# Two streams of a recurrent layer: the output product moved a step later, its result read out by ScalarE and added on GpSimd, the sums of x taken from accumulators

## Chip, cores and metric

The kernel runs on one core of one Trainium2 chip. The metric is the device time of one execution in microseconds. The work per core is divided over five engines with queues of their own, each served in order: TensorE (PE; its weight loads are PEld), VectorE (DVE), ScalarE (ACT), GpSimd (POOL) and SyncE (SP), which here issues the transfers.

## The reference

Sixteen images of 192 channels and 56 x 56 pixels (T = 3136 tokens) go through three recurrent layers and a graph convolution, each with a group norm in front and a residual sum behind. In float32, cut to what matters:

```python
# layers 0 to 2; gn is a group norm over 32 groups
xs = tokens(gn(x))                        # (B, T, C)
k, v, r = xs @ Wk.T, xs @ Wv.T, xs @ Wr.T
fwd = wkv_scan(-exp(w_decay), u, k, v)    # a ratio of two decaying sums along T
bwd = flip(wkv_scan(-exp(w_decay), u, flip(k), flip(v)))
h = sigmoid(r) * 0.5 * (fwd + bwd)
h = (h - mean(h)) * rsqrt(var(h) + eps) * ln_g + ln_b      # over the channels
x = x + image(h @ Wo.T)
# layer 3
xj = max(0, differences of gn(x) to the pixels two rows and two columns away)
x = x + gelu(batchnorm(concat(gn(x), xj) @ conv_w.T + conv_b))
```

The next layer's group norm needs the sums of x and of its squares, for each channel, over all tokens.

## The kernel before

**Tiles.** Images are taken in pairs: a tile of 128 partitions x 3 columns x 448 tokens holds a chunk of one pair (column 0 and 2: the first 128 channels of either image; column 1: the other 64 of both). T is seven chunks. Loops over the three columns go in the order 0, 2, 1.

**Two streams.** The eight pairs form two streams of four. While one stream goes backward through a layer (chunks 6 to 0), the other goes forward (chunks 0 to 6) through its own layer. `steps` is a list written out ahead: each step has at most one backward unit B and one forward unit A (or C, a chunk of the convolution). Chunk 6 of a backward pass stands alone (`backward_alone`), then five or six steps have both: `both_a_first` and five times `both_a` where the forward unit is one of a recurrent layer, `both_c` where it is one of the convolution. The seventh forward chunk follows in `forward_a` or `forward_c`. The plan holds 17 phases of one `both_a_first` and five `both_a` (85 in all), 42 `both_c`, 66 `forward_a`, 24 `backward_alone` and 14 `forward_c`.

**Order.** These functions write the order of instructions out by hand: every engine keeps the order in which they are issued there, and waits with semaphores for the data of others.

**A forward unit.** `a_keys` and `a_values` are products on TensorE, `a_exp` the exponential on ScalarE, `a_ekv` (L885) multiplies by it, `a_q` and `a_p` are scans on VectorE (L836) of the denominator and the numerator, `a_den` and `a_num` add the bonus term (L851, one instruction for columns 0 and 2 and one for column 1, both inputs in SBUF). Ln and Exp on ScalarE (L906, L909) invert the denominator, `a_y` (L913, GpSimd) multiplies. `save` copies a scan's last column for the next chunk (L847 on GpSimd, L845 on ScalarE).

**A backward unit.** `b_gate` and `b_exp` (L934) are the gate's product and exponential, `b_sigmoid` makes the gate of it. `b_q` and `b_p` are the scans the other way, `b_den` and `b_num` their bonus. After the inversion `b_mix` (L969 to L971, GpSimd, nine instructions, all with both inputs in SBUF) makes h. `b_squares` (L978, ScalarE) squares it into the slot of ek, `b_sums` (L985, L987, TensorE) sums h and its squares over channels, `b_rs1` to `b_rs3` make the inverse deviation, `b_spread` (L1009, TensorE) copies it to all partitions, `b_scale` (L1014, VectorE) multiplies h by it. Then the way out:

```python
    def b_x(run, c):
        wob, ps, xs = params[run.l][4], run.ps["o"], run.xb[c]
        for j in ORDER:
            xj = xs.t[:, j, :]
            V.scalar_tensor_tensor(xj, ps[j][:, 0:L], wob[:, column(j)], xj, ALU.add, ALU.add)
```

`b_out` (L591 to L600) is the output product, `b_x` (L1027) adds it and a bias to x and stores x to DRAM (`xd`), and `b_stats` (L722, L723) makes ScalarE pass over x twice, for its sums and those of its squares. `late` notes at which stage a backward chunk stands when its step has ended: 0 (mixed), 0.5 (summed), 1, 2. In `both_a` a chunk mixed in one step is scaled, projected and added in the next.

**Memory.** 33 slots in SBUF hold all tiles of chunk size; a freed slot goes to the end of a list, and the next tile takes the first of the list. A tile's first writer waits until the slot's last reader has ended. Seven PSUM banks are handed out the same way. `gap` and `begin_now` put the steps of the next layer's norm (`norm_sums`, L728, first) between.

Of the kernel before, what the change touches and what calls it, by code (L numbers as in the profile page):

```python
# [39 lines left out]
P = 128  # L40
# [433 lines left out]
def fast_path(ctx: ExitStack, tc: tile.TileContext, flag, x, wproj, wfold, wcfold, wconst, wgroup, sums, picks, vecs, out):  # L474
# [7 lines left out]
    keep = ctx.enter_context(tc.tile_pool(name="fkeep", bufs=1))  # L482
    row = ctx.enter_context(tc.tile_pool(name="frow", bufs=1))
    small = ctx.enter_context(tc.tile_pool(name="fsmall", bufs=4))
    dram = ctx.enter_context(tc.tile_pool(name="fdram", bufs=1, space=bass.MemoryType.DRAM))
    psum = ctx.enter_context(tc.tile_pool(name="fpsum", bufs=1, space=bass.MemoryType.PSUM))
    psconst = ctx.enter_context(tc.tile_pool(name="fpsconst", bufs=1, space=bass.MemoryType.PSUM))
# [6 lines left out]
    def name(s):  # L494
        ngen[0] += 1
        return f"{s}_{ngen[0]}"
# [34 lines left out]
    def column(j):  # L531
        return slice(j % 2, j % 2 + 1)
# [79 lines left out]
    def of(t):  # L612
        return lambda rows, j: t[rows, j, :]
# [100 lines left out]
            self.m, self.ml, self.q, self.p = {}, {}, {}, {}  # L714

    def new_stats():
        return small.tile([P, 2, 3, NL], F32, tag="stats", name=name("stats"))

    def chunk_stats(stats, xt, c):

        for j in ORDER:
            S.activation(junk, xt[:, j, :], AF.Identity, accum_out=stats[:, 0, j, c : c + 1])  # L722
            S.activation(junk, xt[:, j, :], AF.Square, accum_out=stats[:, 1, j, c : c + 1])  # L723


# [198 lines left out]
    def b_gate(run, c):  # L924
        product(run, "r", run.w[2], run.xb[c], c == NL - 1)
        if c == NL - 1:
            take_bias(run, "r", S, -1.0)

    def b_exp(run, c):
        ps, b = run.ps["r"], run.bias["r"]  # L930
        sg = run.sg[c] = Slot("sg")
        for j in ORDER:
            at = j * NL + c
            S.activation(  # L934
                sg.t[:, j, :], ps[j][:, 0:L], AF.Exp, bias=b[:, j, :], scale=-1.0, accum_out=run.chk[:, at : at + 1]
            )
            release(ps[j])
# [57 lines left out]
    def b_rs2(run, c):  # L995
        rs, st = run.rs[c], run.ps["st"]
        V.tensor_sub(rs[HI, :], st[HI, :L], rs[HI, :])  # L997
        release(st)

    def b_rs3(run, c):  # L1000
        rs = run.rs[c]
        S.activation(rs[HI, :], rs[HI, :], AF.Ln, bias=eps4[HI, :])
        S.activation(rs[HI, :], rs[HI, :], AF.Exp, scale=-0.5)  # L1003

    def b_spread(run, c):
        rs = run.rs.pop(c)
        ps = run.ps["rsb"] = banks("rsb")
        for j, rows in ((0, slice(64, 96)), (2, slice(96, P)), (1, HI)):
            PE.matmul(ps[j][:, :L], pick[rows, j, :], rs[rows, :], start=True, stop=True)  # L1009
# [5 lines left out]
            release(ps[j])  # L1015

    def b_out(run, c):
        h = run.h.pop(c)
        run.ps["o"] = banks("ops")
        project(run.ps["o"], params[run.l][5], of(h.t), L)  # L1020
        h.give()

    def b_x(run, c):
        wob, ps, xs = params[run.l][4], run.ps["o"], run.xb[c]
        for j in ORDER:
            xj = xs.t[:, j, :]
            V.scalar_tensor_tensor(xj, ps[j][:, 0:L], wob[:, column(j)], xj, ALU.add, ALU.add)  # L1027
            release(ps[j])
        nc.sync.dma_start(run.dst[c], xs.t)

    def b_stats(run, c):
        xs = run.xb.pop(c)
        chunk_stats(run.new, xs.t, c)
        if c == 0:
            require_all(run.chk, slice(0, NCHK))
            nxt = run.follow
            nxt.stats, nxt.src = run.new, run.dst
            nxt.xa[0] = xs
            begin_later(nxt)
        else:  # L1040
            xs.give()
# [163 lines left out]
    def add(u):  # L1205
        b_x(*u)
        unsummed.append(u)
        del late[u]

    def keys(f):  # L1210
        if f is not None:
            begin_now(f[1])
            if f[0] == "A":
                a_keys(*f[1:])
# [9 lines left out]
    def both_a(b, a, nback, nfront):  # L1224

        den = lambda: a[0].den[a[1]]
        l = of_stage(0.5)
        load_ahead(nback)
        load_ahead(nfront)
        store()  # L1230
        if nback is not None:
            b_gate(*nback[1:])
            b_exp(*nback[1:])
        b_q(*b)
        if l:
            b_rs2(*l)
            b_rs3(*l)
        b_sigmoid(*b)
        a_values(*a)
        if l:  # L1240
            b_spread(*l)
        b_p(*b)
        b_den(*b)
        invert(b[0].ek[b[1]])
        b_num(*b)
        b_mix(*b)
        if l:
            b_scale(*l)
            b_out(*l)
            late[l] = 2  # L1250
        a_ekv(*a)
        sum_up()
        keys(nfront)
        a_q(*a)
        if l:
            add(l)
        b_squares(*b, (0,))
        a_save(*a)
        exp_keys(nfront, (0, 2))
        b_squares(*b, (2,))  # L1260
        exp_keys(nfront, (1,))
        b_squares(*b, (1,))
        b_sums(*b)
        a_p(*a)
        gap()
        a_den(*a)
        b_rs1(*b)
        late[b] = 0.5
        invert(den())
        gap()  # L1270
        a_num(*a)
        a_y(*a)
        gap()

    def both_a_first(b, a, nback, nfront):

        den = lambda: a[0].den[a[1]]
        l = of_stage(0)
        load_ahead(nback)
        load_ahead(nfront)  # L1280
        store()
        a_values(*a)
        b_squares(*l, (0, 2))
        b_q(*b)
        b_sigmoid(*b)
        b_p(*b)
        b_den(*b)
        invert(b[0].ek[b[1]])
        b_num(*b)
        b_mix(*b)  # L1290
        a_ekv(*a)
        b_squares(*l, (1,))
        if nback is not None:
            b_gate(*nback[1:])
            b_exp(*nback[1:])
        b_sums(*l)
        deviation(l)
        a_q(*a)
        keys(nfront)
        spread_and_scale(l)  # L1300
        b_squares(*b, (0,))
        a_save(*a)
        exp_keys(nfront)
        b_squares(*b, (2, 1))
        b_sums(*b)
        a_p(*a, V)
        a_den(*a)
        b_rs1(*b)
        ln(den())
        add(l)  # L1310
        a_num(*a)
        late[b] = 0.5
        exp_minus(den())
        a_y(*a)

    def both_c(b, a, nback, nfront):

# [48 lines left out]
    def forward_a(a, nback, nfront):  # L1366
        l = next(iter(late), None)
        den = lambda: a[0].den[a[1]]
        a_values(*a)
        load_ahead(nback)  # L1370
        ahead = nfront is not None and nfront[1].begun
        if ahead:
            load_ahead(nfront)
        if l and late[l] == 2:
            add(l)
            l = None
        if l and late[l] == 0:
            squares_and_sums(l)
            b_rs1(*l)
            late[l] = 0.5  # L1380
        if l and late[l] == 0.5:
            b_rs2(*l)
            b_rs3(*l)
            late[l] = 1
        if l:
            b_spread(*l)
        elif ahead:
            keys(nfront)
        store()
        a_q(*a)  # L1390
        a_save(*a)
        if ahead and not l:
            exp_keys(nfront)
        a_den(*a)
        gap()
        invert(den())
        a_ekv(*a)
        gap()
        if l:
            b_scale(*l)  # L1400
            if ahead:
                keys(nfront)
                exp_keys(nfront)
            b_out(*l)
            late[l] = 2
        sum_up()
        if nback is not None:
            b_gate(*nback[1:])
        a_p(*a)
        gap()  # L1410
        if l:
            add(l)
            sum_up()
        a_num(*a)
        a_y(*a)
        if nback is not None:
            b_exp(*nback[1:])
        if not ahead:
            load_ahead(nfront)
            keys(nfront)  # L1420
            exp_keys(nfront)
# [231 lines left out]
```

## Time and profile before

| what | us |
|---|---|
| median of 3 runs (lowest, highest) | 5382.33 (5381.34, 5385.62) |
| the profiled execution | 5382.77 |
| its span, first to last instruction | 5381.0 |
| VectorE busy in it | 5014.9 (93%) |
| TensorE busy (ends are modelled) | 4629.7 (86%) |
| ScalarE busy | 3681.2 (68%) |
| GpSimd busy | 2770.3 (51%) |
| granted TensorE clock, mean | 0.916 |

A row of the groups says line, engine, operation, output and inputs, shapes and count, then the busy time, the mean ns of one, and the idle time ahead with what ended it. A row of the timeline says start and length in us, engine, line, operation and count; in brackets the idle time ahead and its releaser. A row of the windows gives, for a stretch, its length and each engine's busy time with its number of instructions, in the order PE, PEld, DVE, ACT, POOL, then the granted clock, DMA's share and GB/s.

### The profile page before, as it was taken

What the parts mean: (1) busy time and instruction counts of PE and PEld (TensorE: products, weight loads), DVE (VectorE), ACT (ScalarE), POOL (GpSimd) and SP (SyncE); (2) the same over time, 40 slices, a digit from 0 to 9 for tenths busy, and PEclk for the clock granted to TensorE, in tenths of its full rate; (3) what the DMA queues carried; (4) which work ended last, traced back from release to release, by engine and by line L of the source; (5) the groups of instructions that cost most, each with busy time, mean ns of one, the idle gap of its engine ahead of it and who ended that gap; (6) DMA issues with size and microseconds to landing.
All of it is one profiled execution on the core that took longest, in us unless ns stands there. A gap on an engine that the chain in (4) does not pass through costs nothing. (4 is left out here: it accounts for less than half of the span.)

```text
span 5381.0 us, 50984 instructions
## 1 busy us (share of the span) xinstructions
PE 4629.7 (86%) x15206; PEld 1498.6 (28%) x15206; DVE 5014.9 (93%) x6556; ACT 3681.2 (68%) x7035; POOL 2770.3 (51%) x2164
## 2 busy tenths in 40 slices
PE   6888988989798898888979888888888988898897
PEld 2222322223232222222323222222222222222222
DVE  6989999999999999999999999999999999999996
ACT  6777667767676676676667767667667566676673
POOL 1555555645454465555444455555535455555463
PEclk8989989989899898998989989999898998999898
DMA  5222212124243212213425121221343312222233
GB/s 149 78 80 72 85 66 88 63 90 140 87 131 89 82 63 73 74 67 105 144 87 150 56 74 67 85 74 62 111 139 94 111 56 74 70 77 80 77 102 115
DMA packets 314271, 482.42 MB, mean 90 GB/s; under 512 B 66432, under 2 KB 306688, under 8 KB 313984
## 3 DMA queue, kind: packets, MB, share of 16 engines
q1 hardware_dynamic: 312832, 477.59, 27.9%
q8 instruction: 123, 2.02, 0.2%
q10 hardware_dynamic: 1152, 1.48, 0.1%
q14 instruction: 164, 1.34, 0.1%
HBM read 324.83 MB, written 154.14 MB: 89 GB/s over the span
## 5 line engine op out<-in xcount | busy, mean ns | idle before, releaser
L913 POOL TENSOR_TENSOR p<-p,q 128x1344 f32<-128x1344 f32 x168 | 510.1, 3037 | 887.8 <-ACT q L909 472.1
L969 POOL TENSOR_TENSOR ekv<-ekv,ek 128x448 f32<-128x448 f32 x504 | 618.2, 1227 | 677.1 <-DVE p L1014 304.9
L836 DVE TENSOR_TENSOR_SCAN p<-fdecays,cp,ekv 128x448 f32<-128x448 f32 x864 | 928.5, 1130 | 7.2 <-POOL p L913 4.5
L836 DVE TENSOR_TENSOR_SCAN q<-fdecays,cq,ek 128x448 f32<-128x448 f32 x864 | 929.2, 1131 | 1.9 <-PE st L987 0.2
L971 POOL TENSOR_TENSOR p<-p,sg 128x448 f32<-128x448 f32 x504 | 599.4, 1189 | 54.5 <-ACT cq L845 10.7
L970 POOL TENSOR_TENSOR p<-p,ekv 128x448 f32<-128x448 f32 x504 | 600.6, 1192 | 39.5
L847 POOL COPY cp<-p 128x3 f32<-128x3 f32 x271 | 196.4, 725 | 686.9 <-DVE p L836 454.3
L978 ACT ACTIVATE ek<-p 128x448 f32<-128x448 f32 x504 | 283.6, 573 | 259.4 <-POOL p L971 257.5
L591 PE MATMUL ops<-p,fwo 128*128 128x448 f32 x336 | 223.5, 755 | 275.3 <-DVE p L1014 275.2
L866 ACT ACTIVATE ek<-k,k 128x448 f32<-128x448 f32 x504 | 292.1, 630 | 243.0 <-PE k L594 216.4
L723 ACT ACTIVATE fjunk<-x 128x448 f32<-128x448 f32 x672 | 387.6, 577 | 21.1
L722 ACT ACTIVATE fjunk<-x 128x448 f32<-128x448 f32 x672 | 384.6, 572 | 14.6
L851 DVE SCALAR_TENSOR_TENSOR q<-ek,fcc,q 128x896 f32<-128x896 f32 x336 | 337.1, 1043 | 51.1 <-ACT cq L845 51.1
L1009 PE MATMUL rsb<-rs,fpicks 32*128 32x448 f32 (+1 forms) x1008 | 335.8, 594 | 48.8 <-ACT rs L1003 46.7
L1027 DVE SCALAR_TENSOR_TENSOR x<-ops,fwob,x 128x448 f32<-128x448 f32 x504 | 315.9, 674 | 52.2 <-PE ops L594 27.1
L851 DVE SCALAR_TENSOR_TENSOR ek<-ek,fcc,q 128x896 f32<-128x896 f32 x336 | 361.6, 1117 | 2.8 <-POOL chk L919 2.8
L851 DVE SCALAR_TENSOR_TENSOR ekv<-ekv,fcc,p 128x896 f32<-128x896 f32 x336 | 330.4, 1024 | 1.2
L934 ACT ACTIVATE sg<-r,r 128x448 f32<-128x448 f32 x504 | 311.9, 624 | 15.8 <-PE r L594 10.4
L885 DVE SCALAR_TENSOR_TENSOR ekv<-v,v,ek 128x448 f32<-128x448 f32 x504 | 312.9, 677 | 0.0
L1014 DVE TENSOR_TENSOR p<-p,rsb 128x448 f32<-128x448 f32 x504 | 281.5, 614 | 31.1 <-PE rsb L1009 31.0
L851 DVE SCALAR_TENSOR_TENSOR p<-ekv,fcc,p 128x896 f32<-128x896 f32 x336 | 293.4, 913 | 10.0 <-POOL cp L847 9.7
L906 ACT ACTIVATE q<-q 128x1344 f32<-128x1344 f32 x168 | 222.4, 1324 | 90.4 <-DVE q L851 65.9
(232 smaller groups left out, 11795.3 us busy)
## 6 DMA issues: line engine op xcount, KB each, us to landing
x<-xd SPq DMA_DIRECT2D x240, 672.0 KB, 5.5
xd<-x SPq DMA_DIRECT2D x168, 672.0 KB, 4.0
x<-in_x_dram SPq DMA_DIRECT2D x320, 224.0 KB, 4.6
x<-in_x_dram SPq DMA_DIRECT2D x320, 112.0 KB, 4.6
out_dram<-ml SPq DMA_DIRECT2D x112, 224.0 KB, 2.3
ring<-xd SPq DMA_DIRECT2D x112, 168.0 KB, 5.3
wkv<-in_wfold_dram SPq DMA_DIRECT2D x24, 640.0 KB, 5.5
out_dram<-ml SPq DMA_DIRECT2D x112, 112.0 KB, 2.3
```

The source lines that it names most:

```text
L722: S.activation(junk, xt[:, j, :], AF.Identity, accum_out=stats[:, 0, j, c : c + 1])
L723: S.activation(junk, xt[:, j, :], AF.Square, accum_out=stats[:, 1, j, c : c + 1])
L836: V.tensor_tensor_scan(s.t[:, j, order], dec[:, column(j)].to_broadcast([P, L]), data.t[:, j, order], init, ALU.mult, ALU.add)
L851: by_channel(lambda js, i: V.scalar_tensor_tensor(dst.t[:, js, :], e.t[:, js, :], cc[:, i : i + 1], state.t[:, js, :], ALU.mult, ALU.add))
L885: V.scalar_tensor_tensor(e.t[:, j, :], ps[j][:, 0:L], b[:, j, :], run.ek[c].t[:, j, :], ALU.add, ALU.mult)
L913: G.tensor_mul(run.h[c].t, run.h[c].t, den.t)
L934: S.activation(sg.t[:, j, :], ps[j][:, 0:L], AF.Exp, bias=b[:, j, :], scale=-1.0, accum_out=run.chk[:, at : at + 1])
L969: G.tensor_mul(y.t[:, j, :], y.t[:, j, :], den.t[:, j, :])
L970: G.tensor_add(h.t[:, j, :], h.t[:, j, :], y.t[:, j, :])
L971: G.tensor_mul(h.t[:, j, :], h.t[:, j, :], sg.t[:, j, :])
L1009: PE.matmul(ps[j][:, :L], pick[rows, j, :], rs[rows, :], start=True, stop=True)
L1027: V.scalar_tensor_tensor(xj, ps[j][:, 0:L], wob[:, column(j)], xj, ALU.add, ALU.add)
```

## The change

In `both_a`, a chunk that was mixed in one step is scaled at the end of the next and projected a step later still (stage 1.5): `b_out` runs early in that step, `b_evict` has ScalarE read the product from PSUM into h, with the bias, and accumulate its sums; `b_add` has GpSimd add h to x, store x, and add the sums of the old x, which `run.stats` holds, to the new sums. The last `both_a` of a phase does this for two chunks. `both_a_first` scales its chunk at the end and leaves it at stage 1.5. In the other steps `b_x` stays on VectorE, with an accumulator output for the sums of x. `b_stats` makes squares only. `both_a`, `both_a_first` and `forward_a` are put in a new order. Statistics get a pool of seven buffers of their own (four before, shared).

```diff
+    def chunk_squares(stats, xt, c):
+        for j in ORDER:
             S.activation(junk, xt[:, j, :], AF.Square, accum_out=stats[:, 1, j, c : c + 1])
...
     def b_x(run, c):
+        run.h.pop(c).give()
...
-            V.scalar_tensor_tensor(xj, ps[j][:, 0:L], wob[:, column(j)], xj, ALU.add, ALU.add)
+            V.scalar_tensor_tensor(
+                xj, ps[j][:, 0:L], wob[:, column(j)], xj, ALU.add, ALU.add, accum_out=run.new[:, 0, j, c : c + 1]
+            )
...
+    def b_evict(run, c):
+        wob, ps, h = params[run.l][4], run.ps["o"], run.h[c].t
+        for j in ORDER:
+            S.activation(
+                h[:, j, :], ps[j][:, 0:L], AF.Identity, bias=wob[:, column(j)], accum_out=run.new[:, 0, j, c : c + 1]
+            )
+            release(ps[j])
+
+    def b_add(run, c):
+        h, xs = run.h.pop(c), run.xb[c]
+        G.tensor_add(xs.t, xs.t, h.t)
+        h.give()
+        nc.sync.dma_start(run.dst[c], xs.t)
+        new = run.new[:, 0, :, c : c + 1]
+        G.tensor_add(new, new, run.stats[:, 0, :, c : c + 1])
...
     def b_stats(run, c):
         xs = run.xb.pop(c)
-        chunk_stats(run.new, xs.t, c)
+        chunk_squares(run.new, xs.t, c)
...
+    def add_evicted(u):
+        b_add(*u)
+        unsummed.append(u)
+        del late[u]
```

`both_a` after the change, whole:

```python
        den = lambda: a[0].den[a[1]]
        l, o = of_stage(0.5), of_stage(1.5)
        last = nback is None
        load_ahead(nback)
        load_ahead(nfront)
        store()
        b_q(*b)
        b_sigmoid(*b)
        a_values(*a)
        b_p(*b)
        sum_up()
        b_rs2(*l)
        b_rs3(*l)
        a_ekv(*a)
        b_out(*o)
        b_den(*b)
        invert(b[0].ek[b[1]])
        b_num(*b)
        b_mix(*b)
        if last:
            b_spread(*l)
            b_scale(*l)
        else:
            b_gate(*nback[1:])
        b_evict(*o)
        if not last:
            b_exp(*nback[1:])
        b_squares(*b, (0,))
        a_q(*a)
        a_save(*a)
        keys(nfront)
        if last:
            b_out(*l)
        b_squares(*b, (2,))
        exp_keys(nfront)
        a_p(*a)
        gap()
        if not last:
            b_spread(*l)
        a_den(*a)
        gap()
        ln(den())
        a_num(*a)
        b_squares(*b, (1,))
        exp_minus(den())
        b_sums(*b)
        b_rs1(*b)
        add_evicted(o)
        if last:
            b_evict(*l)
            add_evicted(l)
        else:
            b_scale(*l)
            late[l] = 1.5
        a_y(*a)
        gap()
        late[b] = 0.5
```

The other two functions, where their order changes:

```diff
     def both_a_first(b, a, nback, nfront):
...
         deviation(l)
+        keys(nfront)
         a_q(*a)
-        keys(nfront)
-        spread_and_scale(l)
         b_squares(*b, (0,))
         a_save(*a)
         exp_keys(nfront)
-        b_squares(*b, (2, 1))
-        b_sums(*b)
+        b_spread(*l)
+        b_squares(*b, (2,))
         a_p(*a, V)
         a_den(*a)
+        ln(den())
+        a_num(*a)
+        b_squares(*b, (1,))
+        exp_minus(den())
+        b_sums(*b)
         b_rs1(*b)
-        ln(den())
-        add(l)
-        a_num(*a)
+        b_scale(*l)
+        late[l] = 1.5
+        a_y(*a)
         late[b] = 0.5
-        exp_minus(den())
-        a_y(*a)
...
     def forward_a(a, nback, nfront):
...
+        if l:
+            if late[l] == 0.5:
+                b_rs2(*l)
+                b_rs3(*l)
+            b_spread(*l)
+            a_den(*a)
+            invert(den())
+            sum_up()
+            a_ekv(*a)
+            b_scale(*l)
+            b_out(*l)
+            if nback is not None:
+                b_gate(*nback[1:])
+            if ahead:
+                keys(nfront)
+                exp_keys(nfront)
+            a_p(*a)
+            a_num(*a)
             add(l)
             sum_up()
```

More of the change, by code (lines that the diff above doesn't have):

```diff
@@ L484, in fast_path @@
     small = ctx.enter_context(tc.tile_pool(name="fsmall", bufs=4))
+    statistics = ctx.enter_context(tc.tile_pool(name="fstats", bufs=7))
     dram = ctx.enter_context(tc.tile_pool(name="fdram", bufs=1, space=bass.MemoryType.DRAM))
@@ L716, in new_stats @@
     def new_stats():
-        return small.tile([P, 2, 3, NL], F32, tag="stats", name=name("stats"))
+        return statistics.tile([P, 2, 3, NL], F32, tag="stats", name=name("stats"))
     def chunk_stats(stats, xt, c):
@@ L722, in chunk_stats @@
             S.activation(junk, xt[:, j, :], AF.Identity, accum_out=stats[:, 0, j, c : c + 1])
+        chunk_squares(stats, xt, c)
+    def chunk_squares(stats, xt, c):
+        for j in ORDER:
             S.activation(junk, xt[:, j, :], AF.Square, accum_out=stats[:, 1, j, c : c + 1])
@@ L1017, in b_out @@
     def b_out(run, c):
-        h = run.h.pop(c)
         run.ps["o"] = banks("ops")
-        project(run.ps["o"], params[run.l][5], of(h.t), L)
-        h.give()
+        project(run.ps["o"], params[run.l][5], of(run.h[c].t), L)
     def b_x(run, c):
+        run.h.pop(c).give()
         wob, ps, xs = params[run.l][4], run.ps["o"], run.xb[c]
@@ L1226, in both_a @@
         den = lambda: a[0].den[a[1]]
-        l = of_stage(0.5)
+        l, o = of_stage(0.5), of_stage(1.5)
+        last = nback is None
         load_ahead(nback)
@@ L1230, in both_a @@
         store()
-        if nback is not None:
-            b_gate(*nback[1:])
-            b_exp(*nback[1:])
         b_q(*b)
-        if l:
-            b_rs2(*l)
-            b_rs3(*l)
         b_sigmoid(*b)
         a_values(*a)
-        if l:
-            b_spread(*l)
         b_p(*b)
+        sum_up()
[3 more added lines that the diff above has]
+        b_out(*o)
         b_den(*b)
@@ L1246, in both_a @@
         b_mix(*b)
-        if l:
+        if last:
+            b_spread(*l)
             b_scale(*l)
-            b_out(*l)
-            late[l] = 2
-        a_ekv(*a)
-        sum_up()
-        keys(nfront)
-        a_q(*a)
-        if l:
-            add(l)
-        b_squares(*b, (0,))
-        a_save(*a)
-        exp_keys(nfront, (0, 2))
+        else:
+            b_gate(*nback[1:])
+        b_evict(*o)
+        if not last:
+            b_exp(*nback[1:])
+        b_squares(*b, (0,))
+        a_q(*a)
+        a_save(*a)
+        keys(nfront)
+        if last:
+            b_out(*l)
         b_squares(*b, (2,))
-        exp_keys(nfront, (1,))
-        b_squares(*b, (1,))
-        b_sums(*b)
+        exp_keys(nfront)
         a_p(*a)
         gap()
+        if not last:
+            b_spread(*l)
         a_den(*a)
-        b_rs1(*b)
-        late[b] = 0.5
-        invert(den())
-        gap()
-        a_num(*a)
+        gap()
+        ln(den())
[3 more added lines that the diff above has]
+        b_sums(*b)
+        b_rs1(*b)
+        add_evicted(o)
+        if last:
+            b_evict(*l)
+            add_evicted(l)
+        else:
+            b_scale(*l)
+            late[l] = 1.5
         a_y(*a)
         gap()
+        late[b] = 0.5
     def both_a_first(b, a, nback, nfront):
@@ L1297, in both_a_first @@
         deviation(l)
+        keys(nfront)
         a_q(*a)
-        keys(nfront)
-        spread_and_scale(l)
         b_squares(*b, (0,))
@@ L1303, in both_a_first @@
         exp_keys(nfront)
-        b_squares(*b, (2, 1))
-        b_sums(*b)
+        b_spread(*l)
+        b_squares(*b, (2,))
         a_p(*a, V)
         a_den(*a)
+        ln(den())
+        a_num(*a)
+        b_squares(*b, (1,))
+        exp_minus(den())
+        b_sums(*b)
         b_rs1(*b)
-        ln(den())
-        add(l)
-        a_num(*a)
+        b_scale(*l)
+        late[l] = 1.5
+        a_y(*a)
         late[b] = 0.5
-        exp_minus(den())
-        a_y(*a)
     def both_c(b, a, nback, nfront):
@@ L1380, in forward_a @@
             late[l] = 0.5
[L1381 to L1387, printed above, removed]
+        if not l and ahead:
             keys(nfront)
@@ L1391, in forward_a @@
         a_save(*a)
[L1392 to L1398, printed above, removed]
-        if l:
+        if l:
+            if late[l] == 0.5:
+                b_rs2(*l)
+                b_rs3(*l)
+            b_spread(*l)
+            a_den(*a)
+            invert(den())
+            sum_up()
+            a_ekv(*a)
             b_scale(*l)
+            b_out(*l)
+            if nback is not None:
+                b_gate(*nback[1:])
             if ahead:
@@ L1403, in forward_a @@
                 exp_keys(nfront)
[L1404 to L1411, printed above, removed]
+            a_p(*a)
+            a_num(*a)
             add(l)
             sum_up()
-        a_num(*a)
+        else:
+            if ahead:
+                exp_keys(nfront)
+            a_den(*a)
+            gap()
+            invert(den())
+            a_ekv(*a)
+            gap()
+            sum_up()
+            if nback is not None:
+                b_gate(*nback[1:])
+            a_p(*a)
+            gap()
+            a_num(*a)
         a_y(*a)
```

## The prediction

> **What bounds the kernel now.** I read the page's busy totals first, then a table of windows one step long, then the timeline of VectorE, GpSimd and ScalarE inside one step, and last the waits.
>
> ```profile
> PE 4629.7 (86%) x15206; PEld 1498.6 (28%) x15206; DVE 5014.9 (93%) x6556; ACT 3681.2 (68%) x7035; POOL 2770.3 (51%) x2164
> ```
> ```profile
> 453.60:478.90 25.30, 22.41 (x80) 6.94 (x78) 25.24 (x31) 19.16 (x36) 15.20 (x12) 1.00 0.17 56
> ```
>
> The second line is one steady step of `both_a`: 25.30 us, in which VectorE works 25.24 and TensorE 22.41. The plan holds 17 phases with one `both_a_first` and five `both_a` steps each, so 102 of the 168 backward chunks pass there; elsewhere (42 `both_c`, 17 forward steps after a phase, `backward_alone`) chunks keep the old way out. So in `both_a` a VectorE microsecond is a microsecond of the kernel. The next fence is one such step, VectorE with GpSimd between, in order of time:
>
> ```profile
> 408.35 1.72 DVE L851 SCALAR_TENSOR_TENSOR ek<-ek,fcc,q 128x896 f32<-128x896 f32 x2
> 409.99 1.74 DVE L851 SCALAR_TENSOR_TENSOR ekv<-ekv,fcc,p 128x896 f32<-128x896 f32 x2
> 412.86 1.14 POOL L969 TENSOR_TENSOR ekv<-ekv,ek 128x448 f32<-128x448 f32 x1 [3.34 <-DVE p L1014]
> ...
> 418.16 1.84 DVE L1027 SCALAR_TENSOR_TENSOR x<-ops,fwob,x 128x448 f32<-128x448 f32 x3
> 419.92 3.22 DVE L836 TENSOR_TENSOR_SCAN p<-fdecays,cp,ekv 128x448 f32<-128x448 f32 x3
> ...
> 422.32 1.14 POOL L971 TENSOR_TENSOR p<-p,sg 128x448 f32<-128x448 f32 x1
> 423.06 1.95 DVE L851 SCALAR_TENSOR_TENSOR q<-ek,fcc,q 128x896 f32<-128x896 f32 x2
> ```
>
> Read: `b_den`, `b_num`, then GpSimd's nine-instruction mix (412.86 to 423.46, 10.60 us), then the sum that is to leave VectorE, then `a_p` and `a_den`. `a_den` begins where the mix ends, and overlaps only its last 0.4 us. What an overlap costs is seen once per phase, where `both_a_first` meets the mix of the step ahead:
>
> ```profile
> 571.00 3.25 DVE L851 SCALAR_TENSOR_TENSOR ek<-ek,fcc,q 128x896 f32<-128x896 f32 x2
> 574.17 3.51 DVE L851 SCALAR_TENSOR_TENSOR ekv<-ekv,fcc,p 128x896 f32<-128x896 f32 x2
> ...
> 571.78 1.99 POOL L969 TENSOR_TENSOR ekv<-ekv,ek 128x448 f32<-128x448 f32 x1
> 573.85 1.40 POOL L970 TENSOR_TENSOR p<-p,ekv 128x448 f32<-128x448 f32 x1
> 575.33 1.87 POOL L971 TENSOR_TENSOR p<-p,sg 128x448 f32<-128x448 f32 x1
> ```
>
> The same four instructions that take 3.30 us free (408.35 to 411.65) take 6.61 (571.00 to 577.61): **3.3 us lost**, on both engines. Last, a wait for a slot, in the first phase:
>
> ```profile
> 252.83 3.23 DVE L836 TENSOR_TENSOR_SCAN p<-fdecays,cp,ekv 128x448 f32<-128x448 f32 x3 [2.00 <-POOL p L913]
> ```
>
> The scan takes its data from no GpSimd product `p`: it waits because its output slot was last read by the previous step's `a_y`. The steps of that phase take up to 29.6 us.
>
> **What the skill says.** The Trainium skill, "SBUF — State Buffer", Who interferes with whom: a VectorE instruction with two SBUF inputs contends with a GpSimd instruction that reads SBUF; one with a single SBUF input does not. The trace agrees: scans (decays lie in PSUM) and L1027 (PSUM plus `x`) keep their time under the mix, the four above double. "Perfetto Trace Analysis", Optimizing Scalar/DVE Operations, warns that moving work between GpSimd and VectorE might not help for that reason. The same page, Identifying Performance Opportunities, takes equal bubbles as a possible sign of too few buffers; the 2.00 us agree. "VectorE: DVE Perf Modes", Two Vector instructions with no wait between them: an accumulator output makes a second instruction; no run here shows its price.
>
> **The change, part by part.**
>
> *VectorE.* 102 x 3 instructions L1027 go. Start to start the three take 1.76 us (418.16 to 419.92), so a step falls from 25.32 (401.27 to 426.59) to 23.56 if nothing else happens.
>
> *ScalarE.* 306 evictions come; nearest row L934 (PSUM in, bias, accumulator): 624 ns plus a 196 ns readout, 0.62 from start to start. 504 identities of L722 go, 0.70 each with readout. In `both_a` that is level (19.2 us of ScalarE per step, cover over 4 us); elsewhere it saves 2.1 us per chunk on ScalarE.
>
> *GpSimd.* 102 additions of 128x1344, like L913 3.04 us, and 102 of 128x3 (L919: 0.20). Per step 15.2 + 3.2 = 18.4 us.
>
> *TensorE.* Same count. `b_out` uses a product scaled a step earlier; its wait on the scaling (2.92 us at 412.31) goes, and the four projections (4.5 us each), spread (2.0) and sums (2.15) make 22.2: it stays below VectorE.
>
> *SP.* The store of `xd` now waits for the addition, some 4 us into the next step, and that step's loads queue behind it. Landing takes about 5 us and TensorE wants the keys' input at about 14: hidden.
>
> *The order.* This decides. Between `b_num` and `a_den` VectorE had scale 1.59, ekv 1.78, `a_q` 3.14, sum 1.76 and `a_p` 3.14. Now scale is at the end, ekv ahead of `b_den`, the sum gone: 6.28 are left. From the start of `b_den`, the mix still begins at +4.51 (Ln and Exp, 408.35 to 412.86) and lasts to +15.11, but `a_den` comes at 1.64 + 1.66 + 6.28 = **+9.58, five mix instructions too early**. `a_den` and `a_num`, four instructions, meet it in full: +3.3, less the 0.21 that `a_den` already lost. Step: 23.56 - 0.21 + 3.3 = **26.65**, 1.33 over today.
>
> *Slots.* `h` lives a step longer, so of the 33 slots some two to six are free where three to nine were. Following the free list, first in first out, the first backward scan of the second and of the third `both_a` step of a phase gets the slot of `ek`, whose last reader is the previous step's sums on TensorE; all of VectorE's step is queued behind that scan. New step: q 3.27, p 3.16, rs 0.65, ekv 1.78, so `b_den` at 8.86, mix from 13.37; it loses some 2.2 to the four (three of its instructions took 5.42 instead of 3.5) and ends at 26.2. Square, sums and their end cost 1.73 more (423.46 to 425.19): the scan starts at **27.9**, past VectorE's 26.65. In the other steps the slot comes from the mix or earlier and is free in time. `b_p` waits for the addition (mix end + 4.2; wanted at + 5.0) and ekv for `a_y` (+ 7.5; wanted + 8.8): both just hidden. In the first phase two scans wait for `a_y` instead: 26.2 + 7.6 = 33.8 against 29.2 now.
>
> *Sum over `both_a`.* 16 phases x (2 x 2.6 + 2 x 1.33 + 1.2 for the last step, where scale sits between and four still meet the mix) = 145; first phase about 12. **+157.**
>
> *Around it.* `both_a_first`: sum out 1.76, `a_den` now meets the mix's last instruction (0.5): -1.3 x 17 = -22. Forward step and `backward_alone`: at 549.59 to 553.79 sums of `x` hold the next layer's norm up for 4.2 us; half of them go (-2.1), and `a_num` ahead of the last sum covers 0.9 of its two waits on TensorE (1.1 and 0.75); one contention of `a_den` there (2.56 us at 532.36) stays in another form: -3 x 17 = -51, bounds 0 and -85. 198 remaining L1027 get accumulators: below nothing has no reason; above, ScalarE's 0.19 each, 38; mostly hidden: +10. ScalarE's relief in `both_c`: 0 to -20, take -5.
>
> Total 157 - 22 - 51 + 10 - 5 = **+89** on the profiled execution's 5382.77 (span 5381.0; median of the runs 5382.33, the same within 0.5): **5472 us**.
>
> **The rivals.**
>
> *The port costs little (faster).* If `a_den` and `a_num` passed the mix free, a step would be 23.56, or 26.2 - 2.2 + 1.73 = 25.7 in the two that wait for sums, or 24.1 for the mix alone: 2 x 0.4 - 3 x 1.2 = -2.8 per phase, -48, with the surroundings' -68 about -115: **5268**. For it: only the two-input instructions are touched. Against: 571.00. The point from which it decides: at under some 1.4 us lost per step in place of 3.3 the whole is faster.
>
> *VectorE alone counts.* No contention, no slot wait: 102 x 1.76 + 68 = -248, **5135**. Against it: the 2.00 us slot wait.
>
> *Deeper starvation.* If a lower granted clock makes the sums later, or the additions push `a_y` into `b_den`, another 1.5 us in each of 85 steps: **5600**. For: by the layout TensorE idles some 4 us ahead of the sums' second half, and steps with a granted clock of 0.93 (428.3 to 453.6) hold 23.7 us of TensorE in place of 22.4. Against: v, wanted at 7.08, would come by about 5.
>
> *It doesn't do what it says:* excluded, 306 instructions leave VectorE.
>
> **How the numbers follow.** Main case 0.66, deeper starvation 0.10, port cheap 0.16, VectorE alone 0.03, ends cancelling 0.05. About 0.2% (11 us) can be told from no change. Slower 0.76, same 0.05, faster 0.19. Main alone: 5390 to 5550 (transitions' bounds, contention 2.4 to 3.5 us). The range leaves out most of the faster cases and the far end of starvation: 5340 to 5575.
>
> **What would show it.** VectorE steps near 26.7 and 27.9; `a_den` and `a_num` together near 6.6 us beside a mix of over 12; a wait of the first backward scan on TensorE's sums, about 1.3 us, in about 34 steps; less wait of the norm on ScalarE's sums. Steps below 25.3, or `a_den` pairs near 3.3, would make it wrong.

## The result: 5838.59 us, slower than forecast

The changed kernel takes **5838.59 us** (5837.69 to 5839.36, four runs) beside 5381.84 for the kernel before on the same chip: ratio 1.085, 95% interval 1.0831 to 1.0869. The forecast was 5472, with 5575 as its upper end: the sign was right, the size was not. Of a loss of 457 us, 89 were worked out.

The page's line of busy times, and the windows row of one steady step of `both_a` (columns as explained above):

```profile
PE 4870.6 (83%) x15206; PEld 1531.7 (26%) x15206; DVE 5208.3 (89%) x6448; ACT 3504.7 (60%) x6639; POOL 3116.8 (53%) x2368
```
```profile
468.50:499.74 31.24, 26.15 (x80) 7.60 (x78) 27.60 (x28) 18.55 (x35) 18.58 (x15) 0.95 0.22 67
```

VectorE has fewer instructions than before and is busy for 193 us more; in a step it works 27.60 us and stands still for 3.6. Before, a step was 25.30 with 25.24 busy. All 17 phases show it: no step of `both_a` is under 31.2. In the table a step is the time from the end of one `a_num` to the end of the next, in the profiled execution:

| us | before | after | difference, all |
|---|---|---|---|
| `both_a`, the first four of a phase (68) | 25.53 | 31.40 | +399 |
| `both_a`, the last (17) | 25.55 | 31.25 | +97 |
| forward step after a phase (17) | 18.76 | 17.15 | -27 |
| `backward_alone` with `both_a_first` (17) | 45.49 | 43.34 | -37 |
| other forward steps (42) | 12.90 | 13.67 | +32 |
| stretches with the convolution (6) | 201.96 | 200.75 | -7 |

The sum is +457. The timeline of VectorE at the end of a step, from `a_den` on, and of GpSimd beside it, first of before (the copy and `a_num`), then of after:

```profile
423.40 1.05 POOL L847 COPY cp<-p 128x3 f32<-128x3 f32 x1
424.93 1.73 DVE L851 SCALAR_TENSOR_TENSOR p<-ekv,fcc,p 128x896 f32<-128x896 f32 x2
```

```profile
467.92 3.21 DVE L856 SCALAR_TENSOR_TENSOR q<-ek,fcc,q 128x896 f32<-128x896 f32 x2
474.71 4.52 DVE L856 SCALAR_TENSOR_TENSOR p<-ekv,fcc,p 128x896 f32<-128x896 f32 x2 [3.58 <-POOL cp L852]
479.15 1.67 DVE L1019 TENSOR_TENSOR p<-p,rsb 128x448 f32<-128x448 f32 x3
```
```profile
468.79 1.86 POOL L976 TENSOR_TENSOR p<-p,sg 128x448 f32<-128x448 f32 x1
470.61 1.52 POOL L974 TENSOR_TENSOR ekv<-ekv,ek 128x448 f32<-128x448 f32 x1
...
473.42 1.13 POOL L976 TENSOR_TENSOR p<-p,sg 128x448 f32<-128x448 f32 x1
474.49 0.19 POOL L852 COPY cp<-p 128x3 f32<-128x3 f32 x1
474.64 3.05 POOL L1049 TENSOR_TENSOR x<-x,p 128x1344 f32<-128x1344 f32 x1
477.64 1.05 POOL L1053 TENSOR_TENSOR stats<-stats,stats 128x3 f32<-128x3 f32 x1
479.40 3.04 POOL L918 TENSOR_TENSOR p<-p,q 128x1344 f32<-128x1344 f32 x1 [0.71 <-DVE p L856]
```

Read: `a_den` runs beside the mix and ends at 471.13. `a_num` could follow, but it writes over the scan p, and the scan's last column must first be saved for the next chunk. GpSimd does that (L852, 0.19 us), in its order behind the mix, which ends at 474.55. So VectorE waits 3.58 us for a copy of three columns. Then the addition to x, next in GpSimd's queue, starts with `a_num` (474.64 and 474.71), and the two instructions of `a_num` take 4.52 us in place of 1.73. In the list of waits, first of before, then of after (total, times, longest):

```profile
DVE p L851 <- POOL cp L847: 9.7, 31, 1.2
```
```profile
DVE p L856 <- POOL cp L852: 283.5, 118, 3.6
```

The dependence was there before, too, and cost 9.7 us in all, 8.3 of them in the other forward steps. In `both_a`, `a_p` ended about when the mix did, so the copy came to a GpSimd that was just free and ran under `a_den` (423.40 to 424.45). After, 273 of the 283.5 us lie in the 85 steps of `both_a`. Over all chunks the page's groups of costly instructions show `a_num` at 1614 ns (913 before):

```profile
L856 DVE SCALAR_TENSOR_TENSOR p<-ekv,fcc,p 128x896 f32<-128x896 f32 x336 | 529.1, 1614 | 283.5 <-POOL cp L852 283.5
```

### The profile page after: what moved, and what is told of

It reads as the page before. It is cut to its first block, busy times and chain, and to the rows that moved or that the text cites. A ratio compares the mean times of both kernels' runs of the same rounds, so it can differ in the third digit from the quotient of the medians.

```text
span 5837.3 us, 51306 instructions
## 1 busy us (share of the span) xinstructions
PE 4870.6 (83%) x15206; PEld 1531.7 (26%) x15206; DVE 5208.3 (89%) x6448; ACT 3504.7 (60%) x6639; POOL 3116.8 (53%) x2368
## 5 line engine op out<-in xcount | busy, mean ns | idle before, releaser
L856 DVE SCALAR_TENSOR_TENSOR p<-ekv,fcc,p 128x896 f32<-128x896 f32 x336 | 529.1, 1614 | 283.5 <-POOL cp L852 283.5
L976 POOL TENSOR_TENSOR p<-p,sg 128x448 f32<-128x448 f32 x504 | 641.3, 1272 | 46.1 <-ACT sg L914 7.9
L852 POOL COPY cp<-p 128x3 f32<-128x3 f32 x271 | 70.8, 261 | 878.0 <-DVE p L841 606.5
L1014 PE MATMUL rsb<-rs,fpicks 32*128 32x448 f32 (+1 forms) x1008 | 387.7, 676 | 172.2 <-ACT rs L1008 112.6
L850 ACT ACTIVATE cq<-q 128x3 f32<-128x3 f32 x312 | 62.6, 201 | 691.3 <-DVE q L841 691.2
L856 DVE SCALAR_TENSOR_TENSOR q<-ek,fcc,q 128x896 f32<-128x896 f32 x336 | 416.6, 1279 | 51.5 <-ACT cq L850 50.9
L728 ACT ACTIVATE fjunk<-x 128x448 f32<-128x448 f32 x672 | 385.4, 573 | 19.1 <-issue 1.2
L992 PE MATMUL st<-p,fsums 128*32 128x448 f32 x672 | 179.0, 614 | 206.4 <-POOL p L976 206.4
L1049 POOL TENSOR_TENSOR x<-x,p 128x1344 f32<-128x1344 f32 x102 | 313.2, 3070 | 5.1 <-ACT p L1042 5.1
L911 ACT ACTIVATE ek<-ek 128x1344 f32<-128x1344 f32 x168 | 221.2, 1317 | 156.6 <-DVE ek L856 156.6
```

Source lines behind the costliest of these rows:

```text
L856: by_channel(lambda js, i: V.scalar_tensor_tensor(dst.t[:, js, :], e.t[:, js, :], cc[:, i : i + 1], state.t[:, js, :], ALU.mult, ALU.add))
L976: G.tensor_mul(h.t[:, j, :], h.t[:, j, :], sg.t[:, j, :])
L1049: G.tensor_add(xs.t, xs.t, h.t)
```

## The experiments

The theory after the result: per step 3.6 us of wait for the save, 2.8 of addition under `a_num`, and 1.3 more of mix under `a_den`. The rivals: the slot wait of the forecast, TensorE, VectorE's own work. Line numbers differ by a few between the kernels, the names of the tiles don't. Ratios are to the kernel before; steps are counted as in the table.

### e1: the save on VectorE

```diff
 # both_a of the changed kernel
-        a_p(*a)
+        a_p(*a, V)
```

> The changed kernel with one edit: in both_a the last column of a_p's scan is copied by VectorE, not GpSimd. Theory (a wait that the prediction left out): a_num writes in place over the scan that GpSimd's copy reads, and that copy is queued behind the mix; with the copy on VectorE the 3.6 us wait of a_num goes from 85 steps, and what is left is the predicted layout: a_den and a_num contend with the mix for the port (+3.3 us a step), so steps of 26.7 us, or 27.9 us in the two of five whose first scan waits for the sums: 31.24 - 26.7 = 4.5 in three, 3.3 in two, 20 us a phase, 17 phases, 342 us: about 5500 us. Rival (slots): the shortage of slots holds the step up and the wait of a_num only takes its place: the time stays above 5750 us and VectorE's first scan shows long waits. Rival (the addition on GpSimd): the 3.9 us of a_num's first instruction is the larger part and stays, about 5600 us.

Measured: 5585.25 us, ratio 1.0388 (1.0371 to 1.0406). One argument takes off 253 us, of the 342 that the theory gave it. Two windows, a step that the slot holds and one that it doesn't, and the timeline of the first one's end, VectorE and GpSimd:

```profile
437.58:466.10 28.52, 25.17 (x78) 7.77 (x78) 26.69 (x30) 18.54 (x35) 18.69 (x14) 0.94 0.24 73
494.78:521.50 26.72, 23.37 (x78) 7.27 (x78) 26.62 (x29) 18.57 (x35) 18.73 (x14) 1.00 0.15 52
```
```profile
459.45 0.70 DVE L852 COPY cp<-p 128x3 f32<-128x3 f32 x1
460.07 2.61 DVE L856 SCALAR_TENSOR_TENSOR q<-ek,fcc,q 128x896 f32<-128x896 f32 x2
462.60 3.50 DVE L856 SCALAR_TENSOR_TENSOR p<-ekv,fcc,p 128x896 f32<-128x896 f32 x2
466.02 1.67 DVE L1019 TENSOR_TENSOR p<-p,rsb 128x448 f32<-128x448 f32 x3
469.58 3.23 DVE L841 TENSOR_TENSOR_SCAN q<-fdecays,cq,ek 128x448 f32<-128x448 f32 x3 [1.89 <-PE st L992]
```
```profile
465.69 1.40 POOL L976 TENSOR_TENSOR p<-p,sg 128x448 f32<-128x448 f32 x1
467.05 3.04 POOL L1049 TENSOR_TENSOR x<-x,p 128x1344 f32<-128x1344 f32 x1
```
```profile
DVE q L841 <- PE st L992: 60.0, 33, 2.3
```

This is the layout of the forecast: a step of 26.72 (26.65 forecast), `a_den` and `a_num` under the mix, and in the second and third step of a phase the first scan waiting for TensorE's sums, 33 times (34 forecast). That the step fits to 0.1 us is in part chance: the pair takes 6.0 us together (460.07 to 466.10), which is 2.7 more than free and not 3.3, and the rest is VectorE's copy, slowed by the mix (0.70), which the forecast didn't have. The edit also takes the addition off `a_num`, which now ends (466.10) before the addition starts (467.05), and meets the end of the mix instead, at 3.50 us. Missed was the last `both_a`, at 31.02: there the scaling moves the pair back until `a_num` meets the first of the two additions. In this step the rival of the addition was right, and the whole came nearer to its 5600 than to the 5500 of the theory.

### e5: no addition on GpSimd

```diff
 # b_add of the changed kernel
-        G.tensor_add(xs.t, xs.t, h.t)
```

> The changed kernel with GpSimd's addition of h to x left out of b_add (the residual of those 102 chunks is not added; everything else, the save of the last column on GpSimd too, stays). Theory: in the changed kernel a_num waits 3.6 us for GpSimd's copy of the scan's last column, which stands behind the mix, and then takes 3.9 instead of 1.15 us because the addition (3.05 us) starts with it. Without the addition the wait stays and the length goes: a_num's first instruction near 1.2 us, a steady step 28.4 us in place of 31.2, the kernel near 5600 us (5560 to 5650). Rival: the length of a_num belongs to the wait and the mix, not to the addition: step 31, kernel 5800 or more.

This kernel leaves out the residual sum of 102 chunks; it is for timing alone. Measured: 5584.0 us, ratio 1.0385 (1.0368 to 1.0402); steps 28.5 us. The timeline of `a_den` and `a_num`:

```profile
454.97 3.23 DVE L856 SCALAR_TENSOR_TENSOR q<-ek,fcc,q 128x896 f32<-128x896 f32 x2
461.78 1.75 DVE L856 SCALAR_TENSOR_TENSOR p<-ekv,fcc,p 128x896 f32<-128x896 f32 x2 [3.59 <-POOL cp L852]
```

The wait stays, the length of `a_num` goes from 4.52 to 1.75: the addition alone makes that length. The two causes are not independent, though. The addition meets `a_num` only because the wait brings it there: e1 takes away the wait and, but for the last step of a phase, the meeting with it. That both edits take off some 254 us is a coincidence: in steps that the slot doesn't hold e1 is shorter (26.7 beside 28.5), in the last step of a phase it is longer (31.0 beside 28.5).

### e6: another slot for the first scan

```diff
 # both_a of e1
+        b_q(*b)
         load_ahead(nback)
         load_ahead(nfront)
         store()
-        b_q(*b)
```

> As e1_save_on_vector (the changed kernel, save of the numerator on VectorE), but in both_a the first backward scan takes its slot ahead of the loads of x instead of behind them. Nothing else moves: the scan gets a slot last read by the mix, and the load gets the one last read by TensorE's sums. Theory: the second and third both_a of a phase (28.2 to 28.7 us in e1) were held by that slot alone; they fall to 26.7 like the others, 34 x 1.7 = 58 us, kernel near 5527 (5510 to 5545), and the waits of the scan on the sums go. Rival: TensorE or the slot of the second scan holds these steps as well, the wait only moves: 5570 to 5590.

Measured: 5516.51 us, ratio 1.026 (1.0243 to 1.0277), 69 us below e1. The same step as in e1's first window, and what is left of the wait:

```profile
434.83:461.53 26.70, 24.01 (x78) 7.42 (x78) 26.60 (x30) 18.57 (x35) 18.71 (x14) 0.94 0.25 78
```
```profile
DVE q L841 <- PE st L992: 0.5, 1, 0.5
```

The slot alone held those steps, not TensorE: a load of x can have the late slot without harm. The last `both_a` stays at 31.09.

### e7: more work between the mix's start and `a_den`

```diff
 # both_a of e6
-        b_rs2(*l)
-        b_rs3(*l)
-        a_ekv(*a)
         b_out(*o)
         b_den(*b)
         invert(b[0].ek[b[1]])
         b_num(*b)
         b_mix(*b)
+        b_rs2(*l)
+        b_rs3(*l)
+        a_ekv(*a)
...
-        add_evicted(o)
         if last:
             b_evict(*l)
-            add_evicted(l)
...
         a_y(*a)
+        add_evicted(o)
+        if last:
+            add_evicted(l)
```

> As e6_slot_order, with two moves in both_a: a_ekv and b_rs2 go from ahead of b_den to behind b_num, so that 2.4 us more lie between the start of the mix and a_den; and the addition to x stands behind a_y on GpSimd instead of ahead of it. Same instructions. Theory (the port is what the change paid): a_den now meets the last three mix instructions instead of five, and a_num of the last both_a no longer meets the two additions: steps 25.9 instead of 26.7, the last one 25 instead of 31.0, kernel 5345 (5310 to 5400). Rival: TensorE, whose sums of h then start later, or the scan's slots, hold the step: steps near 27 and the kernel 5430 to 5500.

Measured: 5398.25 us, ratio 1.0041 (1.0029 to 1.0054). The first four `both_a` of a phase (68 steps) are 25.88, as worked out. The last ones are 27.33, where 25 was expected: the pair runs free there, but the scaling ahead of it waits for TensorE's spread, 1.74 and 0.65 us:

```profile
519.09 1.15 DVE L1019 TENSOR_TENSOR p<-p,rsb 128x448 f32<-128x448 f32 x2 [1.74 <-PE rsb L1014]
520.88 0.62 DVE L1019 TENSOR_TENSOR p<-p,rsb 128x448 f32<-128x448 f32 x1 [0.65 <-PE rsb L1014]
```

A window of a steady step, then VectorE and GpSimd in it:

```profile
426.94:452.50 25.56, 22.74 (x72) 7.14 (x74) 25.46 (x29) 18.21 (x36) 18.48 (x13) 0.93 0.27 82
```
```profile
446.95 0.48 DVE L852 COPY cp<-p 128x3 f32<-128x3 f32 x1
447.35 2.62 DVE L856 SCALAR_TENSOR_TENSOR q<-ek,fcc,q 128x896 f32<-128x896 f32 x2
449.88 2.61 DVE L856 SCALAR_TENSOR_TENSOR p<-ekv,fcc,p 128x896 f32<-128x896 f32 x2
```
```profile
446.27 1.14 POOL L974 TENSOR_TENSOR ekv<-ekv,ek 128x448 f32<-128x448 f32 x1
447.49 2.00 POOL L975 TENSOR_TENSOR p<-p,ekv 128x448 f32<-128x448 f32 x1
449.56 1.40 POOL L976 TENSOR_TENSOR p<-p,sg 128x448 f32<-128x448 f32 x1
```

Two mix instructions are left for the pair to meet, and it still takes 5.14 in place of 3.30: no order of the changed kernel tried here keeps them apart in the first four steps. Still, e1, e6 and e7 together take 440 us off the changed kernel with the same work on the same engines, but for the copy: nearly the whole loss was the order. What is left is 78 us more than e3, which has the accumulators alone.

### e9: a shorter mix

```diff
 # b_mix of e7
             G.tensor_add(h.t[:, j, :], h.t[:, j, :], y.t[:, j, :])
-            G.tensor_mul(h.t[:, j, :], h.t[:, j, :], sg.t[:, j, :])
```

> As e7_mix_earlier_apart, with the third of the mix's three operations (the multiplication by the gate, L976, three of the nine instructions) left out everywhere; the gate is made but not multiplied in. Theory (a VectorE step of 23.6 us and the port above it): the mix now ends 3.4 us sooner, about when a_den begins, so the four two-input instructions run free: steps 23.6 to 23.9 in place of 25.6 to 25.9, kernel 5398 less 68 x 2.0 and some 20 for the last steps and the surroundings, near 5240 (5210 to 5270). Rival: with the port free, TensorE or the slots hold the step: steps stay at 25 and more, kernel 5330 to 5390.

This kernel makes the gate and leaves its multiplication out; it is for timing alone. Measured: 5160.51 us, ratio 0.9588 (0.9572 to 0.9604), lower than expected since the shorter mix also takes 67 us off the stretches with the convolution and 36 off `backward_alone` with `both_a_first`. The first four steps of a phase take 23.95 on average; the last, at 27.84, gained nothing. What the experiment was for is the steady step, with the end of the mix below it:

```profile
413.71:437.31 23.60, 21.75 (x78) 6.76 (x70) 23.50 (x30) 18.49 (x36) 13.97 (x10) 1.00 0.29 89
```
```profile
432.01 1.13 POOL L975 TENSOR_TENSOR p<-p,ekv 128x448 f32<-128x448 f32 x1
433.84 0.17 DVE L852 COPY cp<-p 128x3 f32<-128x3 f32 x1
433.91 1.74 DVE L856 SCALAR_TENSOR_TENSOR q<-ek,fcc,q 128x896 f32<-128x896 f32 x2
435.57 1.74 DVE L856 SCALAR_TENSOR_TENSOR p<-ekv,fcc,p 128x896 f32<-128x896 f32 x2
```

With GpSimd silent under the pair, the step is 23.60, where the forecast had put VectorE's own work at 23.56. The 1.76 us that the change takes off VectorE are real, and in e7 the meeting with GpSimd takes them back. That TensorE and the slots would allow such a step with the whole mix is not shown: the shorter mix also lets the sums of h start earlier.

### e2: the kernel before, its sum later

```diff
 # both_a of the kernel before
-        if l:
-            add(l)
         b_squares(*b, (0,))
...
         a_num(*a)
+        if l:
+            add(l)
```

> The kernel before with one edit: in both_a VectorE adds the output product to x after a_num instead of between a_q and a_p; not one instruction more or less. a_den then comes 1.76 us earlier, while two instructions of the mix are left. Theory (port and in-place wait): a_den's two instructions lose some 1.5 us to the mix, and a_num waits up to 1.5 us more for GpSimd's copy behind it: 27 us in place of 25.3 in 85 steps, about +150 us: 5530 us. Rival (VectorE's work alone sets the step): 5382 us, within 0.3%.

Measured: 5495.51 us, ratio 1.0217 (1.02 to 1.0234): 116 us lost with the same instructions, only in another order. `a_den` starts while the mix runs and takes 3.40 us (1.95 in the kernel before, at 423.06). The second line is the last of the mix:

```profile
448.86 3.40 DVE L851 SCALAR_TENSOR_TENSOR q<-ek,fcc,q 128x896 f32<-128x896 f32 x2
449.90 1.88 POOL L971 TENSOR_TENSOR p<-p,sg 128x448 f32<-128x448 f32 x1
```

So VectorE's sum, in its old place, kept `a_den` off the mix; its 1.76 us were partly cover. The loss is under the 150 us of the theory, which also had `a_num` wait up to 1.5 us for the copy: it waits 0.2.

### e3: accumulators only

```diff
 # the kernel before
-            V.scalar_tensor_tensor(xj, ps[j][:, 0:L], wob[:, column(j)], xj, ALU.add, ALU.add)
+            V.scalar_tensor_tensor(
+                xj, ps[j][:, 0:L], wob[:, column(j)], xj, ALU.add, ALU.add, accum_out=run.new[:, 0, j, c : c + 1]
+            )
...
-        chunk_stats(run.new, xs.t, c)
+        for j in ORDER:
+            S.activation(junk, xs.t[:, j, :], AF.Square, accum_out=run.new[:, 1, j, c : c + 1])
```

> The kernel before, with the sums of x taken from an accumulator output of VectorE's additions in all 504, and ScalarE making squares alone. Theory: both_a stays at 25.3 us (VectorE's readout of the accumulator, 0.08 us in the trace of the changed kernel, hides); backward_alone gains 2.1 us where the next norm waits for the sums, 17 to 24 times: -36 to -50 us, about 5340 us. Rival (ScalarE's sums were hidden): 5382 us. Rival (readouts cost VectorE 0.08 us each on its path): +25 us in both_a, about 5370 us.

Measured: **5320.16 us**, ratio 0.9892 (0.9875 to 0.9908): 1.1% faster than the kernel before, and more than the 36 to 50 us expected. `both_a` stays at 25.54; 39 us of the gain lie at the phases' ends, in `backward_alone` with `both_a_first`, where the norm waited for the last chunk's sums, 11 in the other forward steps and 10 in the stretches with the convolution. The row of that wait in the kernel before, and the two rows that stand in its place in e3's list (one wait, of 16 to 20 us, is in both):

```profile
DVE mv L728 <- ACT fjunk L723: 77.5, 19, 20.6
```
```profile
DVE mv L728 <- ACT fjunk L1036: 18.3, 18, 1.1
DVE mv L728 <- ACT fjunk L723: 16.6, 1, 16.6
```

### e4 and e10: the order of the forward steps

e4 is e3 with the changed kernel's order of `forward_a` after a phase of `both_a`; `forward_a_tail`, not shown, holds that order:

```diff
 # forward_a of e3
+        if l and late[l] == 0.5:
+            return forward_a_tail(a, l, nback, nfront, ahead)
```

> As the kernel before with accumulators, and in forward_a the new order of the change, for the forward step behind a phase of both_a alone (17 steps). Theory: 1.6 us less in each, 18.76 to 17.15 as the traces of both kernels show: -27 us against the run with accumulators alone, about 5313 us. Rival: the 1.6 us came from the emptier queue behind the slower both_a, not from the order: no gain, about 5340 us.

Measured: 5320.72 us, ratio 0.9893 (0.9876 to 0.9909), no gain over e3. The forward step falls from 18.95 to 15.28, 62 us in all, but `backward_alone` with `both_a_first` behind it grows from 43.21 to 46.05, 48 us, and the stretches with the convolution by 12. The rival had no gain either, but for another reason: it took the shorter step for an effect of the slower `both_a`. The order does shorten the step; the time comes back behind it.

e10 is e7 with the opposite exchange, the old order in all other forward steps.

> As e7_mix_earlier_apart, but forward_a in the order of the kernel before wherever the step doesn't follow a both_a (it keeps the new order after one). Theory: the new order costs 46 us in the 42 other forward steps (577 in place of 531 in the kernel before with accumulators), above all in the six that follow a convolution, where the output product stands ahead of the keys: kernel 5352 (5340 to 5365), steps of both_a unchanged. Rival: as in e4 the time only moves to the next wait: 5380 or more. Either way above the 5320 of e3, since a step of 25.9 is no shorter than the 25.5 there.

Measured: 5373.58 us, ratio 0.9985 (0.9978 to 0.9992), of a theory that said 5352. The forward steps give back their 46 us (577 to 531), as the theory had it, but the convolution's stretches take 25 more (1198 to 1223): about half of the time only moved, as the rival had it. Why these stretches take more stays open.

### e8 and e11: ScalarE and GpSimd, but in the same step

e8 is e3 with eviction and addition in place of VectorE's sum, without the step's delay; the keys' product goes ahead of the output product, and the save is on VectorE:

```diff
 # both_a of e3
             b_scale(*l)
-            b_out(*l)
-            late[l] = 2
         a_ekv(*a)
         sum_up()
         keys(nfront)
+        if l:
+            b_out(*l)
         a_q(*a)
-        if l:
-            add(l)
...
         b_sums(*b)
-        a_p(*a)
+        if l:
+            b_evict(*l)
+        a_p(*a, V)
...
         a_y(*a)
+        if l:
+            add_evicted(l)
```

> The kernel before with the sums of x from accumulators (e3) and, in both_a, ScalarE's eviction and GpSimd's addition in place of VectorE's sum, but without the step's delay: product, eviction and addition stay in the step in which h is scaled, the keys' product goes ahead of the output product, the addition stands behind a_y, the save is on VectorE. Theory: VectorE alone would be at 23.7 us a step, but a_den comes 1.8 us earlier, into the last two instructions of the mix, and loses about what it gained: 25.3 to 25.8, kernel 5300 to 5340, no gain over e3 (5320). Rival: VectorE's own work counts: steps of 23.8, kernel near 5180. Second rival: the addition runs into b_den of the next step as well, 27 us, kernel 5430.

Measured: 5755.79 us, ratio 1.0706 (1.0688 to 1.0724): none of the three expectations. The largest of TensorE's waits:

```profile
PE k L592 <- DMA x<-xd: 501.4, 64, 10.3
```

The store of the added x waits for the addition, and SP's queue holds the next step's loads behind that store: so TensorE waits for the keys' x. e11 tests this reading; it issues the store behind the loads (in the last step of a phase, at the step's end) and changes nothing else:

```diff
 # both_a of e8; b_add only notes the store
         load_ahead(nback)
         load_ahead(nfront)
+        put_away()
         store()
```

> As e8_eviction_same_step, but in both_a the store of the added x is issued behind the next step's loads of x instead of ahead of them; all else as there. In e8 TensorE waited 501 us in 64 places for the keys' x: SP's queue held the loads behind a store that waits for GpSimd's addition. Theory: with the store behind, that wait is gone, and what is left is VectorE's 23.7 plus the port: a_den meets the last two mix instructions, and the addition ends about when b_den begins: steps 25.3 to 26, kernel 5310 to 5350, level with e3 (5320). Rival: ScalarE holds it all the same (the eviction waits for a product that stands behind the keys, b_rs1 and the inversion stand behind the eviction, and so the addition still meets b_den): steps 27 and more, kernel above 5420.

Measured: 5550.73 us, ratio 1.0322 (1.0305 to 1.0339). TensorE's wait for x is gone from the list, 205 us with it, and the rival of e11 is what remains. The steady step is 27.6 us. GpSimd and VectorE about its start:

```profile
666.28 3.04 POOL L914 TENSOR_TENSOR p<-p,q 128x1344 f32<-128x1344 f32 x1 [5.79 <-ACT q L910]
669.27 3.05 POOL L1045 TENSOR_TENSOR x<-x,p 128x1344 f32<-128x1344 f32 x1
```
```profile
669.61 4.26 DVE L852 SCALAR_TENSOR_TENSOR ek<-ek,fcc,q 128x896 f32<-128x896 f32 x2
673.80 1.74 DVE L852 SCALAR_TENSOR_TENSOR ekv<-ekv,fcc,p 128x896 f32<-128x896 f32 x2
```

`a_y` comes late, by ScalarE, and pushes the addition into `b_den`: 4.26 us in place of 1.74. The first `both_a` of a phase, which meets no earlier addition, takes 25.1. The difference of 2.5 us is what `b_den` loses in that meeting.

## Why the prediction was right or wrong

**The step that failed** is the cost of `a_den` and `a_num`: "four instructions, meet it in full: +3.3". It priced `a_num` as an instruction that only competes with the mix. It left out that `a_num` writes in place over p, whose last column GpSimd still has to copy, and that this copy is queued behind the nine mix instructions, in the midst of which the new order lets the scan end. What the runs show in its place: `a_den` at 3.21 under the mix where before had 1.95 (+1.26), the wait for the copy (+3.58), `a_num` at 4.52 under the addition for 1.73 (+2.79). With 23.56 they make 31.19; the step has 31.24. The third follows from the second: without the wait, `a_num` is over when the addition starts. e5 takes the third away alone, 255 us; e1 takes the second and, in all but the last step of a phase, the third, and lets `a_num` meet the mix (3.50): 253 us. The forecast counted GpSimd's time, 18.4 us a step, and placed the addition and `a_y` in its queue, but not the copy. The wait row of L847, with 31 waits, stood in the trace of before and was not read.

**What was right in it:** VectorE's saving (23.60 in e9); that the four lose time where they meet the mix (2.7 us in e1, where 3.3 was forecast; that the step fits all the same is chance, since the copy made up for it); the slot wait, its steps and its cause (28.52 for 27.9; e6 takes it away). That the change is slower was no luck: with the wait for the copy gone, the first four steps still take 27.9 (e1) and 27.0 (e6) for 25.5 before. In the changed kernel itself TensorE's sums hold no first scan: the longer step gives TensorE time. In the first phase alone three scans wait 7.4 us each, for GpSimd's mix, where the forecast had `a_y`.

**The last step of a phase** was sized at +1.2 and measured +5.7: the scaling between is no help to `a_num`, which waits for the copy (2.4 us) and meets the addition there as well (4.52). In e1 and e6 it still meets the first addition.

**SP** was put down as hidden, and is in the changed kernel: its list of TensorE's waits has no transfer of x. e8 shows what it costs where the addition is a little later.

**Around `both_a`:** -73 forecast for `both_a_first`, `backward_alone` and the forward step after a phase, -64 measured. Not forecast: +32 in the other forward steps, from the new order of `forward_a` (e10 gives 46 back there, and takes 25 elsewhere). The accumulators outside `both_a` were put at +10; e3, with them everywhere, gains some 60 us, of which 39 lie at the phases' ends, where the forecast had part of it in its -51. The other 20 have the other sign: ScalarE's relief seems to be worth more than the readouts cost, though no run separates the two. That the new order of the forward step adds to it is not seen in e4.

**The rivals:** "VectorE alone counts" and "the port costs little" fall with e1 and e7. "Deeper starvation" came nearest in time, at 5600, but neither of its mechanisms is what the trace shows: TensorE is not late, and `a_y` ends (482.44) well ahead of `b_den` (489.57).

## What to carry to other kernels

When an instruction is moved forward on one engine, list all that it waits for, the readers of what it overwrites included, and find where each stands in its own engine's queue at the new time: a copy of 0.19 us behind a block of 10 us is a wait for what is left of the block. Where VectorE has two inputs in SBUF and GpSimd reads SBUF, too, add their times as if they were one engine. It is a rule of thumb drawn from these runs: here 6.6 us of such instructions and 16.7 of mix, addition and `a_y` (10.6 and 2 x 3.04) would fill 23.3 of a step of 23.6, and no order tried here kept them apart in the steady steps. And test the parts of a change one by one: its smallest part, the accumulators of e3, is the only one that gained by itself.

## What the runs showed of the hardware

Two-input VectorE instructions that met a GpSimd addition of 3.05 us lost nearly all of its length: 2.5 us in e11, 2.8 in the changed kernel. Against the mix, whose instructions take 1.13 us alone, a pair of them lost 0.9 us (e7, `a_num`) to 1.8 (e1, `a_num`).

VectorE's copy of three columns takes 0.17 us where GpSimd is silent (e9) and 0.48 (e7) or 0.70 (e1) beside the mix; in e7 it ends at 447.43, as the GpSimd instruction that began before it does (447.41). The Trainium skill, "SBUF — State Buffer", Who interferes with whom, says that a copy can run in a mode with two ports and then stands still while GpSimd holds the shared pair; these times agree, even for three columns, though no run here shows the mode itself. GpSimd's own copy takes 1.02 in place of 0.19 beside `b_den` (e7, 434.86).

The accumulator output of VectorE's sum adds an instruction of 0.08 us (198 of them, 16.0 us in all) that hardly shows from start to start: 0.60 us in e7 (549.18 to 549.78), 0.59 before.
